# Last expert of a mixture of experts: the order in which four tiles take their gathered rows on VectorE

## The chip, the core and the metric

The kernel runs on one core of one Trainium2 chip. The time is the device time of one execution in microseconds (us); "the time" of a kernel is the median of several runs. Besides the times there is a profile: one execution recorded by the hardware profiler. Its engines are PE (TensorE matmuls), PEld (TensorE weight loads), DVE (VectorE), ACT (ScalarE), POOL (GpSimd) and SP (SyncE, which issues most DMAs).

## What is computed

One decoder layer, in float32, on 16 sequences of 256 tokens with 256 channels. Three steps, each followed by a residual sum and a layer norm: a recurrence over time with a gated state, an attention of the tokens over a context of 77 rows and themselves, and a mixture of experts. Only the last matters here:

```python
weights = _router(x, expert_embeddings)
ones = (weights > 0).astype(weights.dtype)
cap_ones = jnp.where(jnp.cumsum(ones, axis=0) <= expert_capacity, ones, 0.0)
caw = weights * cap_ones
vals, idx = jax.lax.top_k(caw.T, expert_capacity)
index = idx.reshape(-1)
x_flat = x.reshape(n_tokens, hidden)
tokens = x_flat[index].reshape(E, expert_capacity, hidden)
inter = jax.nn.relu(jnp.einsum('ech,eih->eci', tokens, first_linear))
out = jnp.einsum('eci,ehi->ech', inter, second_linear)
out = out * vals[:, :, None]
final = jnp.zeros((n_tokens, hidden), x.dtype).at[index].add(out.reshape(-1, hidden))
```

The router's weights are a softmax over each token's best 2 of 8 experts, and an expert takes at most 512 rows. A token has up to two experts. Its output row is the layer norm of its input row plus the weighted results of both.

## The kernel before

The attention takes most of the span; the experts come at the end, in a loop of nine turns (lines 1394 to 1415). Turns 0 and 1 belong to expert 0 (four tiles of 128 rows, and two more), turns 2 to 8 to experts 1 to 7 with four tiles each. `LAST` is 8. Each turn has these parts:

- The token rows were put into a DRAM buffer `xg`, sorted by expert. `Rows(e)` (line 1144) loads a turn's rows, and `read` (line 1157) works out, for every row, the weight `w`, whether another expert's result joins it (`joins`), where that lies (`at`), and to which output row it goes (`to`; out of bounds where a later expert finishes the token).
- `turn_rows` (line 1227) transposes the rows on PE, `first_product` (line 1240) makes the hidden layer in four matmul groups, with ScalarE's Relu (line 1255).
- `second_product` (line 1264) makes 128 x 256 of output for each tile with four accumulated matmuls (line 1275). In turns before the last, ScalarE scales each by its weight (line 1285), and for every two tiles SP stores them into the DRAM buffer `oe` (line 1288), from which later experts' turns gather them. In the last turn, VectorE instead first puts "input row plus joined row" of all four tiles into `y` (line 1271, through `add_other`, line 1262), and then adds each product with its weight (line 1283). Its tiles 2 and 3 have PSUM banks of their own (`pk`, `pq`).
- `gather(e + 1)` (line 1305) issues, on POOL, one indirect DMA for each tile of the next turn (line 1310). It reads what this turn stored, so the first waits for that store.
- `finish` (line 1318) takes the tiles in groups: statistics (line 1334) and aggregate (line 1335) of each tile, variance plus epsilon (line 1338), `root` (line 1291: ScalarE's square root at line 1294, then four small VectorE instructions that take the reciprocal and refine it, lines 1296 to 1302), the scaling of each tile (line 1342), and one indirect DMA for each tile to the output, issued by POOL (line 1343). In the last turn the groups are tiles 0 and 1, tile 2, tile 3.

The order on each engine is made when the program is built. The framework gives every engine a queue of its own; what is traced earlier goes first if it is ready by the builder's estimate, otherwise something later may take its place. `with tc.issue_after(ins):` is the means to constrain that: what is traced in the block is queued behind `ins`. Line 1410 uses it in turn 7: its `finish` stands in a block behind the last gather of turn 8.

Of the kernel before, what the change touches and what calls it, by code (L numbers as in the profile page):

```python
# [10 lines left out]
F32 = mybir.dt.float32  # L11
I32 = mybir.dt.int32
AF = mybir.ActivationFunctionType
ALU = mybir.AluOpType
# [4 lines left out]
P = 128  # L19
B, S, D = 16, 256, 256  # L20
# [18 lines left out]
def decoder_layer(  # L39
# [29 lines left out]
    V, A, G, T = nc.vector, nc.scalar, nc.gpsimd, nc.tensor  # L69
# [5 lines left out]
    NS = CAP // P  # L75
# [8 lines left out]
    def bank(name, tag="mm", bufs=2):  # L84
        return ps.tile([P, 512], F32, tag=tag, bufs=bufs, name=name)
# [40 lines left out]
    def apart(group, dma):  # L126

        for other in groups.get(group, []):
            tc.declare_no_dep(dma.ins, other.ins, reason="disjoint rows")
        groups.setdefault(group, []).append(dma)  # L130
# [3 lines left out]
    def rsqrt(v, n, rows, name):  # L134
        r = small.tile([P, n], F32, tag="r", name=f"r{name}")
        powers.append(G.tensor_tensor(r[:rows], v[:rows], nhalf[:rows, 0:n], ALU.pow))
        return r
# [674 lines left out]
    rows, xets = {}, {}  # L812
# [322 lines left out]
    LAST = E  # L1135
    SLOTS = [(0, 0, NS), (0, CAP, GT)] + [(e, FIRST[e], NS) for e in range(1, E)]
# [90 lines left out]
    def turn_rows(e):  # L1227
        x, n = rows[e].x, rows[e].n
        xet = e0.tile([P, DC, CAP], F32, tag="xet", bufs=2, name=f"xet{e}")
        for k in range(DC):  # L1230
            pt = bank(f"pe{e}_{k}", "pk" if k == 0 else "pq", 1)
            for s in range(n):
                T.transpose(pt[:, s * P : (s + 1) * P], x[:, s, k * P : (k + 1) * P], ident)  # L1233
            if k == 0:
                V.tensor_copy(xet[:, k, 0 : n * P], pt[:, 0 : n * P])
            else:
                A.copy(xet[:, k, 0 : n * P], pt[:, 0 : n * P])
        xets[e] = xet

    def first_product(e):  # L1240
        xet, w1, c = xets.pop(e), w1_s[SLOTS[e][0]], SLOTS[e][2] * P
        it = e0.tile([P, NF, CAP], F32, tag="it", name=f"it{e}")
        for f in range(NF):
            if f == 0:
                two = ps.tile([P, 2, 512], F32, tag="s", bufs=1, name=f"pi{e}")
            pi = two[:, f, :] if f < 2 else bank(f"pi{e}_{f}", "pa" if f == 2 else "po", 1)
            for k in range(DC):
                T.matmul(  # L1248
                    pi[:, 0:c],
                    lhsT=w1[:, k, f * P : (f + 1) * P],  # L1250
                    rhs=xet[:, k, 0:c],
                    start=(k == 0),
                    stop=(k == DC - 1),
                )
            A.activation(it[:, f, 0:c], pi[:, 0:c], AF.Relu)
        return it

    gs, ys = {}, {}

    def add_other(e, s, dst, src):  # L1260

        V.scalar_tensor_tensor(dst, gs[e][:, s, :], rows[e].joins[:, s : s + 1], src, ALU.mult, ALU.add)

    def second_product(e, it, tiles):
        if tiles[0] == 0:
            ys[e] = e2.tile([P, NS, D], F32, tag="ye", name=f"ye{e}")
        y = ys[e]
        w2 = w2_s[SLOTS[e][0]]
        if e == LAST and tiles[0] == 0:
            for s in range(NS):  # L1270
                add_other(e, s, y[:, s, :], rows[e].x[:, s, 0:D])
        for s in tiles:
            po = bank(f"pf{e}_{s}") if e < LAST or s < 2 else bank(f"pf{e}_{s}", ("pk", "pq")[s - 2], 1)
            for f in range(NF):
                T.matmul(  # L1275
                    po[:, 0:D],
                    lhsT=it[:, f, s * P : (s + 1) * P],
                    rhs=w2[:, f, :],
                    start=(f == 0),
                    stop=(f == NF - 1),  # L1280
                )
            if e == LAST:
                V.scalar_tensor_tensor(y[:, s, :], po[:, 0:D], rows[e].w[:, s : s + 1], y[:, s, :], ALU.mult, ALU.add)  # L1283
                continue
            A.activation(y[:, s, :], po[:, 0:D], AF.Copy, scale=rows[e].w[:, s : s + 1])  # L1285
            if s % 2 == 1:
                r0 = SLOTS[e][1] + (s - 1) * P
                nc.sync.dma_start(oe_d[r0 : r0 + 2 * P, :].rearrange("(i p) d -> p i d", p=P), y[:, s - 1 : s + 1, :])
        return y

    def root(v, n, name):

        q = es.tile([P, n], F32, tag="qe", name=f"qe{name}")
        A.activation(q, v, AF.Sqrt)
        i0 = es.tile([P, n], F32, tag="ie", name=f"ie{name}")
        V.reciprocal(i0, q)
        i2 = es.tile([P, n], F32, tag="i2", name=f"i2{name}")
        V.tensor_tensor(i2, i0, i0, ALU.mult)
        t = es.tile([P, n], F32, tag="te", name=f"te{name}")
        V.scalar_tensor_tensor(t, i2, -0.5, v, ALU.mult, ALU.mult)  # L1300
        r = es.tile([P, n], F32, tag="re", name=f"re{name}")
        V.scalar_tensor_tensor(r, t, 1.5, i0, ALU.add, ALU.mult)
        return r

    def gather(e):

        R = rows[e]
        gs[e] = e2.tile([P, NS, D], F32, tag="ge", name=f"ge{e}")
        for s in range(R.n):
            last = G.indirect_dma_start(  # L1310
                out=gs[e][:, s, :],
                out_offset=None,
                in_=oe_d[0 : SLOTS[e][1], :],
                in_offset=bass.IndirectOffsetOnAxis(ap=R.at[:, s : s + 1], axis=0),
            )
        return last

    def finish(e, y):
        R = rows[e]
        mv = es.tile([P, NS, 2], F32, tag="mve", name=f"mve{e}")  # L1320
        o = e2.tile([P, NS, D], F32, tag="oe", name=f"oe{e}")
        us = {}
        for a, z in [(0, 2), (2, 3), (3, 4)] if e == LAST else [(a, a + 2) for a in range(0, R.n, 2)]:
            for s in range(a, z):
                if e == LAST:
                    u = y[:, s, :]
                else:
                    u = es.tile([P, D], F32, tag="u", name=f"ue{e}_{s}")
                    V.tensor_tensor(u, R.x[:, s, 0:D], y[:, s, :], ALU.add)
                    if e > 1:  # L1330
                        add_other(e, s, u, u)
                us[s] = u
                st = small.tile([P, 6], F32, tag="st", name=f"ste{e}_{s}")
                V.bn_stats(st, u)  # L1334
                V.bn_aggr(mv[:, s, :], st)  # L1335
            n = z - a
            v = small.tile([P, n], F32, tag="v", name=f"ve{e}_{a}")
            V.tensor_scalar(v, mv[:, a:z, 1], EPS, None, ALU.add)
            r = rsqrt(v, n, P, f"e{e}_{a}") if e == 0 else root(v, n, f"{e}_{a}")
            for s in range(a, z):  # L1340
                i = slice(s - a, s - a + 1)
                V.tensor_scalar(o[:, s, :], us[s], mv[:, s, 0:1], r[:, i], ALU.subtract, ALU.mult)  # L1342
                dma = G.indirect_dma_start(  # L1343
                    out=out_f,
                    out_offset=bass.IndirectOffsetOnAxis(ap=R.to[:, s : s + 1], axis=0),
                    in_=o[:, s, :],
                    in_offset=None,
                    bounds_check=N - 1,
                    oob_is_err=False,
                )  # L1350
                apart("out", dma)


    heads = [(b, h) for b in range(B) for h in range(H)]
# [36 lines left out]
    e2 = ctx.enter_context(tc.tile_pool(name="e2", bufs=2))  # L1391
    load_expert(1, e2)
    load_expert(2, e2)
    for e in range(LAST + 1):
        it = first_product(e)
        if e < LAST:
            rows[e + 1] = Rows(e + 1)
            rows[e + 1].read(e + 1)

        tiles = list(range(SLOTS[e][2]))  # L1400
        ahead = 1 if e == 1 else 0
        if ahead:
            second_product(e, it, tiles[:ahead])
        if 0 < e < LAST:
            turn_rows(e + 1)
        y = second_product(e, it, tiles[ahead:])
        gathered = gather(e + 1) if 0 < e < LAST else None
        if e == LAST - 1:

            with tc.issue_after(gathered.ins):  # L1410
                finish(e, y)
        else:
            finish(e, y)
        if 2 <= e < E - 1:
            load_expert(e + 1, e2)

# [49 lines left out]
```

## Time and profile before

| what | value |
|---|---|
| time, median of 3 runs | 1169.77 us |
| the three runs | 1169.77, 1172.89, 1169.11 us |
| the profiled execution's own time | 1171.0 us |
| its span | 1169.3 us |
| granted TensorE clock, mean | 0.997 |
| DVE busy, of the span | 782.1 us (67%) |
| POOL busy, of the span | 316.1 us (27%) |
| turn 8's second matmuls (line 1275) | 1151.94 to 1159.01 us |
| turn 8's four gather issues (line 1310) start | 1149.04, 1150.31, 1151.57, 1152.82 us |
| turn 7's four output issues (line 1343) start | 1154.07, 1155.39, 1156.69, 1157.97 us |
| turn 8's four output issues start | 1161.39, 1162.66, 1163.94, 1165.22 us |

Positions are microseconds from the start of the span. The profiled execution's own time is a little above its span, by what lies around the recorded instructions. A row of the timeline gives the start, the length, the engine, the line, the operation, and output and inputs by the names of the program; in brackets stands the idle time of that engine before it, and what ended it. "issue" there means that the engine waited for nothing that the profile shows. The chain of work that ended last is followed back from the last instruction: each piece is what released the next one.

### The profile page before, as it was taken

How to read it: one execution, taken by the hardware profiler on the slowest of the kernel's cores; microseconds unless marked ns; L12 is line 12 of the kernel's file. 1: busy time of each engine (PE TensorE's matmuls, PEld its weight loads, DVE VectorE, ACT ScalarE, POOL GpSimd, SP SyncE). 2: the span in 40 equal slices, each digit the busy share in tenths (PEclk: the TensorE clock that was granted, in tenths of full speed). 3: DMA queues.
4: the chain of work that ended last, by engine and by line, in shares of the span. 5: the costliest groups of instructions: out<-in, count | busy, mean ns of one | idle time of the engine just before them, and what ended most of it. 6: DMA issues, size and time to landing. Idle time of an engine off the chain costs nothing. (4 is left out here: it accounts for less than half of the span.)

```text
span 1169.3 us, 16020 instructions
## 1 busy us (share of the span) xinstructions
PE 1135.1 (97%) x5380; PEld 821.0 (70%) x5380; DVE 782.1 (67%) x2144; ACT 499.0 (43%) x1315; POOL 316.1 (27%) x565
## 2 busy tenths in 40 slices
PE   7999999999999999999999999999999999999996
PEld 3465676767787777677777777777777778876664
DVE  6655877676657776777567757865567555665666
ACT  3344444453444344444444444444444444523331
POOL 2201241114210530242015302340142014144455
PEclk9999999999999999999999999999999999999998
DMA  8741010001000110010000100000001000046652
GB/s 276 206 128 39 20 38 18 11 28 58 19 12 10 54 36 12 28 40 19 12 10 27 37 11 10 18 19 12 10 17 46 20 10 15 21 159 138 181 160 90
DMA packets 47417, 60.63 MB, mean 52 GB/s; under 512 B 7957, under 2 KB 37374, under 8 KB 47336
## 3 DMA queue, kind: packets, MB, share of 16 engines
q1 hardware_dynamic: 39686, 50.18, 14.1%
q0 software_dynamic: 6048, 9.22, 3.3%
q8 instruction: 42, 0.69, 0.2%
q10 hardware_dynamic: 1602, 0.23, 0.1%
q14 instruction: 39, 0.32, 0.1%
HBM read 36.33 MB, written 30.78 MB: 57 GB/s over the span
## 5 line engine op out<-in xcount | busy, mean ns | idle before, releaser
L660 PE MATMUL po<-ptt,v 128*128 128x256 f32 (+1 forms) x768 | 189.2, 381 | 1.6 <-DVE rs L632 1.6
L660 PEld LDWEIGHTS po<-ptt,v 128*128 128x128 f32 (+1 forms) x768 | 142.0, 190 | 51.7 <-issue 34.4
L609 PE MATMUL pk<-kvt,wkv_s 128*128 128x333 f32 x512 | 165.4, 444 | 0.0
L624 PE MATMUL s<-kt,qt 128*128 128x333 f32 x512 | 164.5, 443 | 0.0
L626 DVE TENSOR_REDUCE nm<-s 128x2 f32<-128x666 f32 x128 | 108.3, 846 | 72.1 <-PE s L624 68.1
L630 ACT ACTIVATE p<-s,nm 128x333 f32<-128x333 f32 x256 | 135.7, 536 | 44.5 <-DVE nm L626 44.2
L614 PE MATMUL pq<-kvt,wq_s 128*128 128x256 f32 x512 | 131.2, 378 | 0.0
L609 PEld LDWEIGHTS pk<-kvt,wkv_s 128*128 128x128 f32 x512 | 91.1, 191 | 45.6 <-issue 22.9
L668 ACT ACTIVATE ot<-po,bkv_s 128x256 f32<-128x256 f32 x128 | 60.9, 476 | 140.3 <-PE po L660 135.7
L624 PEld LDWEIGHTS s<-kt,qt 128*128 128x128 f32 x512 | 96.3, 188 | 31.6 <-issue 1.3
L614 PEld LDWEIGHTS pq<-kvt,wq_s 128*128 128x128 f32 x512 | 96.7, 189 | 30.8 <-issue 1.0
L649 ACT COPY ptt<-pb 77x256 f32<-77x256 f32 x128 | 47.3, 369 | 164.1 <-PE pb L646 161.0
L634 DVE TENSOR_SCALAR p<-p,rs 128x333 f32<-128x333 f32 x256 | 98.5, 421 | 3.3
L990 POOL DMA_INDIRECT xg<-xs,sidx x64 | 66.1, 1032 | 98.3 <-ACT ot L668 38.9
L648 DVE COPY ptt<-pa 128x512 f32<-128x512 f32 x128 | 87.3, 682 | 0.7 <-PE pa L646 0.7
L646 PEld LDWEIGHTS pa<-ident,p 128*128 128x128 f32 x512 | 63.9, 141 | 29.3
L611 ACT ACTIVATE kt<-pk,bkv_s 128x333 f32<-128x333 f32 x128 | 69.1, 540 | 28.2 <-PE pk L609 21.7
L646 PE MATMUL pa<-ident,p 128*128 128x128 f32 x512 | 76.8, 273 | 0.0
L351 DVE SCALAR_TENSOR_TENSOR cv<-hp,cw,cv 128x512 f32<-128x512 f32 (+1 forms) x108 | 74.1, 692 | 1.6
L616 ACT ACTIVATE qt<-pq,bqs 128x256 f32<-128x256 f32 x128 | 61.1, 478 | 20.2 <-PE pq L614 15.3
L336 PE MATMUL ph<-xT,inw 128*128 128x512 f32 (+1 forms) x144 | 63.1, 567 | 5.5 <-DMA inw<-in_in_wT 4.4
L1275 PE MATMUL pf<-w,it 128*128 128x256 f32 x272 | 61.3, 381 | 2.0 <-ACT ye L1285 1.7
(264 smaller groups left out, 1764.6 us busy)
## 6 DMA issues: line engine op xcount, KB each, us to landing
v<-vc SPq DMA_DIRECT2D x16, 308.0 KB
xg<-zero SPq DMA_DIRECT2D x34, 131.0 KB
xe<-xg SPq DMA_DIRECT2D x8, 524.0 KB
xt<-in_x_in SPq DMA_DIRECT2D x16, 256.0 KB
out<-o SPq DMA_DIRECT2D x16, 256.0 KB
w<-in_w1T SPq DMA_DIRECT2D x8, 512.0 KB
w<-in_w2T SPq DMA_DIRECT2D x8, 512.0 KB
oe<-ye SPq DMA_DIRECT2D x15, 256.0 KB
```

Source lines behind the costliest of these rows:

```text
L351: conv = V.scalar_tensor_tensor(cv, hp[:, :, k : k + S], cw[:, c, k : k + 1], cv, ALU.mult, ALU.add)
L609: T.matmul(pk[:, 0:J], lhsT=wkv_s[:, k, f], rhs=kvt[:, k, :], start=(k == 0), stop=(k == DC - 1))
L611: A.activation(kt, pk[:, 0:J], AF.Identity, bias=bkv_s[:, h : h + 1])
L614: T.matmul(pq[:, 0:S], lhsT=wq_s[:, k, f], rhs=kvt[:, k, 0:S], start=(k == 0), stop=(k == DC - 1))
L624: T.matmul(s[:, ic, 0:J], lhsT=qt[:, ic * P : (ic + 1) * P], rhs=kt, start=True, stop=True)
L626: V.tensor_reduce(nm, s[:, :, 0:J], AX.X, ALU.max, negate=True)
L630: A.activation(p[:, ic, :], s[:, ic, 0:J], AF.Exp, bias=nm[:, ic : ic + 1], accum_out=sm[:, ic : ic + 1])
L634: V.tensor_scalar(p[:, ic, :], p[:, ic, :], rs[:, ic : ic + 1], None, ALU.mult)
L646: T.transpose(dst[0:jn, c0 : c0 + P], pn[:, ic, j0 : j0 + jn], ident)
L648: turned = V.tensor_copy(ptt[:, 0:2, :], pt01.rearrange("p (j i) -> p j i", j=2))
L660: T.matmul(po[:, 0:S], lhsT=vs[b][0:jn, jc, h * DH : (h + 1) * DH], rhs=ptt[0:jn, jc, :], start=(jc == 0), stop=(jc == 2),)
L990: dma = G.indirect_dma_start(out=xg[:, :], out_offset=bass.IndirectOffsetOnAxis(ap=sidx[:, t, c : c + 1], axis=0), in_=xs[b + t // GT][:, ...
```

## The change

In the last turn, VectorE's work is laid out in another order. The "input row plus joined row" is made for tiles 0 and 1 alone; then the second product of these two and their `finish` are traced. That of tiles 2 and 3 is queued behind the aggregate of tile 1 (`known`). The second product and the `finish` of tile 2 and then of tile 3 stand in a block that is queued behind the scaling of tile 1 (`scaled`). For that, `finish` takes its groups of tiles as an argument and returns the two instructions, and its tiles are kept between its calls. The other turns get the same groups as before. No instruction is added or taken away.

```diff
     def second_product(e, it, tiles):
-        if tiles[0] == 0:
+        if tiles[0] == 0 and e < LAST:
             ys[e] = e2.tile([P, NS, D], F32, tag="ye", name=f"ye{e}")
         y = ys[e]
         w2 = w2_s[SLOTS[e][0]]
-        if e == LAST and tiles[0] == 0:
-            for s in range(NS):
-                add_other(e, s, y[:, s, :], rows[e].x[:, s, 0:D])
         for s in tiles:
...
-    def finish(e, y):
+    ends_of = {}
+
+    def finish(e, y, groups_of_tiles):
         R = rows[e]
-        mv = es.tile([P, NS, 2], F32, tag="mve", name=f"mve{e}")
-        o = e2.tile([P, NS, D], F32, tag="oe", name=f"oe{e}")
+        if groups_of_tiles[0][0] == 0:
+            ends_of[e] = (
+                es.tile([P, NS, 2], F32, tag="mve", name=f"mve{e}"),
+                e2.tile([P, NS, D], F32, tag="oe", name=f"oe{e}"),
+            )
+        mv, o = ends_of[e]
         us = {}
-        for a, z in [(0, 2), (2, 3), (3, 4)] if e == LAST else [(a, a + 2) for a in range(0, R.n, 2)]:
+        for a, z in groups_of_tiles:
...
-                V.bn_aggr(mv[:, s, :], st)
+                known = V.bn_aggr(mv[:, s, :], st)
...
-                V.tensor_scalar(o[:, s, :], us[s], mv[:, s, 0:1], r[:, i], ALU.subtract, ALU.mult)
+                scaled = V.tensor_scalar(o[:, s, :], us[s], mv[:, s, 0:1], r[:, i], ALU.subtract, ALU.mult)
...
+        return known, scaled
...
+        if e == LAST:
+
+            y = ys[e] = e2.tile([P, NS, D], F32, tag="ye", name=f"ye{e}")
+            other = lambda s: add_other(e, s, y[:, s, :], rows[e].x[:, s, 0:D])
+            other(0)
+            other(1)
+            second_product(e, it, [0, 1])
+            known, scaled = finish(e, y, [(0, 2)])
+            with tc.issue_after(known.ins):
+                other(2)
+                other(3)
+            with tc.issue_after(scaled.ins):
+                for s in (2, 3):
+                    second_product(e, it, [s])
+                    finish(e, y, [(s, s + 1)])
+            break
...
-        gathered = gather(e + 1) if 0 < e < LAST else None
+        gathered = gather(e + 1) if e > 0 else None
+        pairs_of = [(a, a + 2) for a in range(0, SLOTS[e][2], 2)]
         if e == LAST - 1:
 
             with tc.issue_after(gathered.ins):
-                finish(e, y)
+                finish(e, y, pairs_of)
         else:
-            finish(e, y)
+            finish(e, y, pairs_of)
```

## The prediction

> **What bounds the kernel now.** I read the page first, then the chain of work that ended last from 1140 us on, then the timeline of the same stretch, then the waits and the table of stretches.
>
> ```profile
> PE 1135.1 (97%) x5380; PEld 821.0 (70%) x5380; DVE 782.1 (67%) x2144; ACT 499.0 (43%) x1315; POOL 316.1 (27%) x565
> ```
>
> TensorE (PE) is busy for 97% of the span, so nearly all the time is its queue, and the change adds and removes no matmul. What can move is only the stretch behind the last matmul. The chain shows what sets it (start, length):
>
> ```profile
> 1152.82 3.44 DMA ge<-oe,at
> 1156.26 0.02 issue
> 1156.28 0.04 DVE ye L1262
> 1156.32 0.37 issue
> 1156.68 0.49 DVE ye L1283
> ...
> 1163.94 0.98 POOL out L1343
> 1164.92 1.28 POOLq L1462
> ```
>
> From 1152.82 the chain isn't on PE: it waits for the fourth gather, then runs on VectorE (DVE), then through the output DMAs that GpSimd (POOL) issues. The timeline gives the order (start, length, engine, line; in brackets the idle time before it):
>
> ```profile
> 1151.84 0.48 DVE L1262 SCALAR_TENSOR_TENSOR ye<-ge,joins,xe 128x256 f32<-128x256 f32 x1 [1.40 <-DMA ge<-oe,at]
> 1151.94 7.07 PE L1275 MATMUL pf<-w,it 128*128 128x256 f32 x32
> ...
> 1153.12 0.48 DVE L1262 SCALAR_TENSOR_TENSOR ye<-ge,joins,xe 128x256 f32<-128x256 f32 x1 [0.80 <-DMA ge<-oe,at]
> ...
> 1154.85 0.48 DVE L1262 SCALAR_TENSOR_TENSOR ye<-ge,joins,xe 128x256 f32<-128x256 f32 x1 [1.24 <-DMA ge<-oe,at]
> ...
> 1156.28 0.48 DVE L1262 SCALAR_TENSOR_TENSOR ye<-ge,joins,xe 128x256 f32<-128x256 f32 x1 [0.95 <-DMA ge<-oe,at]
> 1156.68 0.48 DVE L1283 SCALAR_TENSOR_TENSOR ye<-pf,we,ye 128x256 f32<-128x256 f32 x1
> ...
> 1157.97 0.97 POOL L1343 DMA_INDIRECT out<-oe,to  x1 [0.30 <-issue]
> ...
> 1161.39 0.97 POOL L1343 DMA_INDIRECT out<-oe,to  x1 [2.44 <-DVE oe L1342]
> ...
> 1165.22 0.97 POOL L1343 DMA_INDIRECT out<-oe,to  x1 [0.30 <-issue]
> ```
>
> Call the four L1262 instructions adds 0 to 3, those of L1283 combines 0 to 3. All four adds stand ahead of combine 0, so tile 0, whose own gather was in at 1151.84, waits until 1156.28 for tile 3's. The table of stretches prices it (length, then busy PE, PEld and DVE):
>
> ```profile
> 1154.07:1156.28 2.21, 2.21 (x12) 1.93 (x12) 0.48 (x1) 0.00 (x0) 1.90 (x2) 1.00 0.41 113
> 1161.39:1164.41 3.02, 0.00 (x0) 0.00 (x0) 2.84 (x16) 0.41 (x2) 2.41 (x3) 0.61 0.20 73
> ```
>
> DVE idles while PE works, and is nearly full once PE is done. POOL idled 2.44 us before the first of the last four output issues, and then the four follow 1.28 us apart (0.98 and 0.30 between): 1161.39 + 3 x 1.28 = 1165.23. So the end is "first output issue plus three pitches"; the last scaling (oe, L1342), done at 1164.41, was 0.5 us early for its issue.
>
> **The change, part by part.**
>
> *Python only.* The moved allocations, `ends_of`, the returned handles, `pairs_of` and `gather` under `e > 0` issue nothing: turn 0 still gathers nothing, turns 1 to 7 do as before. Cost 0, with nothing needed to hide it.
>
> *What the ordering binds.* The trace shows it at line 1410, where turn 7's finish is queued behind the last gather: its POOL issues waited until 1154.07, behind the gathers (1149.04 to 1153.77), while DVE instructions of the same block ran from 1140.45. So only the engine of the named instruction is bound, here DVE. PE's matmuls for tiles 2 and 3 should keep their place.
>
> *When the products can be taken.* Turn 7's second matmuls began at 1138.01 and ScalarE took its tiles at 1139.94, 1141.67, 1143.40 and 1145.64: 1.93, 3.66, 5.39 and 7.63 after. Turn 8's begin at 1151.94: 1153.87, 1155.60, 1157.33, 1159.57. Combines 0 and 1 now wait for PE, which they didn't. Price of that wait: at least 0, at most the 0.5 by which turn 7's fourth tile ran late. I take 0, since the first three were evenly 1.73 apart.
>
> *Tiles 0 and 1 (moved forward).* From rows of before, start to start: combine to statistics 0.52 (1156.68 to 1157.20), statistics to aggregate 0.46, aggregate to ve (L1338) 0.21. Tile 0: 1153.87, 1154.39, 1154.85. Tile 1: 1155.60, 1156.12, 1156.58. This last is `known`. ve follows at 1156.79.
>
> *Adds 2 and 3 (moved back).* They come behind `known`; their gathers were in at 1154.85 and 1156.28, so they wait for no DMA. Each occupies DVE for 0.40 (1159.64 to 1160.04 for an instruction of their shape). The price has two ends. If they fill the holes of the root: from ve to the first scaling takes 1.40 with nothing between (1162.60 to 1164.00), and 1.80 with two instructions of 128x256 and small ones between (1158.92 to 1160.72). If both stand ahead of ve: 0.90 and then 1.40, 0.29 more in all (scaling at 1158.88). I take the fill, since turns 6 and 7 and turn 8 itself were laid out so. First scaling: 1156.79 + 1.80 = 1158.59.
>
> *Tiles 2 and 3 (queued behind the scaling).* Waiting behind it on DVE are combines 2 and 3, their statistics and scalings; through them ScalarE's two roots and two output issues. The next combine follows the first scaling by 0.69 (1160.72 to 1161.41): combine 2 at 1159.28 (before: 1159.64), its product two us old. ve of tile 2: 0.52 + 0.46 + 0.21 later, 1160.47; combine 3 another 0.06 on (1161.35 to 1161.41): 1160.53. From combine 3 I copy the old tail: scaling 2 ended 1.89 after it (1163.30), scaling 3 3.00 after it (1164.41). New: 1162.42 and 1163.53.
>
> *POOL.* Turn 7's outputs still end at 1158.94; the first issue is free from 1159.24, and scaling 0 (done 1158.95) plus the 0.30 pitch gap gives 1159.25. Second 1160.53. Third 1162.42 + 0.30 = 1162.72. Fourth the later of 1163.83 and 1162.72 + 1.28: 1164.00. Before: 1165.22. Sum: -1.22 us. The start from 1165.22 to the span's end, 4.08 us of issue and landing, is kept.
>
> So the stall of 4.4 us before the adds doesn't come back whole: about 2 us of it become work for two tiles, the rest is spent waiting for tile 1's product and on the two adds, now in the crowded part; the bound passes from POOL's pitch to DVE's work for tiles 2 and 3.
>
> *A rule against it.* The new DVE work from 1153.87 lies beside POOL's output issues of turn 7. The Trainium skill (SBUF — State Buffer, sections "SBUF: two separate sides" and "A bandwidth-pool intuition that's wrong (but worth ruling out)") says that GpSimd can't write its DMA descriptors while VectorE runs certain two-port instructions, and gives 620 ns becoming 3100. Were turn 7's four issues held 2.5 us each, the first output of turn 8 would start some 10 us later, about 1169, and the kernel be slower by 8. The trace disagrees for these forms: the gather issues at 1140.82 and 1142.07 ran beside adds (two inputs in SBUF) and took 0.94 and 0.95, and outputs take 0.97 to 1.01; the single long one, 1.25 at 1133.46, lies beside such work too. Even 0.27 on each of the four puts the first output at 1160.33 and the fourth at 1164.17 by pitch, 0.17 later than my sum. I take 0.
>
> **The rivals.**
>
> 1. *My forecast, filled holes* (chance 0.60): -1.22, with adds ahead of ve -0.93. Profiled span 1169.3 to 1168.1, that execution 1171.0 to 1169.8. The median of before is 1169.77, 1.2 below the profiled execution: 1168.55, rounded 1168.6.
>
> 2. *More* (0.10): only PE's end and POOL's pitch bind. Tile 3 visible at 1159.57, then 0.52 + 0.46 + 0.21 + 1.40 + 0.41 + 0.30 gives 1162.87; four pitches from 1159.25 give 1163.09. So -2.1 at most, 1167.6. Against it: DVE has more than that to do for tiles 2 and 3.
>
> 3. *Nothing comes of it* (0.17): tile 1's product late by 0.5, adds ahead of ve (0.3) and an output issue at 1.25 leave -0.3 or so; or the order isn't changed where it counts. Within 0.4 of 1169.8.
>
> 4. *Slower: tiles 2 and 3 in series* (0.11). The queue takes from DVE the work that filled its holes. If tile 3 follows only after tile 2's whole chain, each takes 0.52 + 0.46 + 0.21 + 1.40 + 0.41 = 3.00: 1159.28 + 6.00 = 1165.28, issue 1165.58, +0.36; with the adds ahead of ve +0.65, so 1170.1 to 1170.4. It decides once scaling 3 ends after 1164.92, that is when 1.4 us of overlap are lost. For it: the tiles are traced one after the other. Against it: in turns 6 to 8 other tiles' instructions do stand in the holes.
>
> 5. *The ordering holds PE too* (0.02): matmuls for tile 2 start at 1159.28, tile 3 is visible 3.66 later at 1162.94, +3.00 + 0.30 = 1166.24: +1.0, 1170.8. Line 1410's trace speaks against it.
>
> **How the numbers follow.** About 0.3%, 3.5 us, is what a measurement of this kernel can tell from no change. None of the cases reaches it: even the best is 2.1, the worst 1.0. Outside lie only a disturbance of the time itself (one of the three runs of before was 3.1 above the median) and something that no row shows, the port rule among it: 0.02 faster, 0.05 slower, 0.93 within. The range goes from the bound of case 2, 1167.6, to case 5 less a little, 1170.6, which also leaves room for a median that is some tenths off; below and above remain about 0.08 and 0.12.
>
> **What would show it.** Right: combine 0 near 1153.9 and ended-by PE, not by a gather; adds 2 and 3 between ve and the first scaling; first output issue near 1159.3, directly behind turn 7's last, with idle time of POOL now before the third; the fourth near 1164.0; PE's last matmul still at 1159.0. Wrong: combine 1 after 1156; adds 2 and 3 ahead of ve; combine 3 behind scaling 2 (case 4); PE idle between tiles 1 and 2 (case 5); output issues of turn 7 longer than 1.1 us (the port rule). Anything that differs before 1150 would be none of my steps.

## The result and the profile after

Over 20 runs each, the median went from 1171.04 us (1168.13 to 1173.54) to 1173.12 us (1171.05 to 1177.11): ratio 1.0016, interval 1.0009 to 1.0024. That is slower by 1.9 us by the ratio, 2.1 by the medians. It is less than the 0.3% that the forecast took for no change, but the interval is clear of 1, it lies on the other side of no change than the predicted -1.2 us, and 1173.12 lies above the forecast's range of 1167.6 to 1170.6. An occasion, below, is a set of runs made together. The later runs fell on two kinds of occasion, told apart by their traces: PE's products came in time or late. So every ratio here compares runs of one occasion, and positions are given as "us after turn 8's first second matmul".

| | before | after |
|---|---|---|
| profiled execution, its span | 1171.0, 1169.3 us | 1173.65, 1171.9 us |
| first of turn 8's second matmuls | 1151.94 | 1152.50 |
| fourth output issue, after that | 13.28 us | 15.38 us |

The span grew by 2.6 us. Of that, 0.56 is the later start of the matmuls, upstream of the edit (of the stretches from one turn's second matmuls to the next, only that from turn 6 to turn 7 differs by more than 0.2: 15.36 against 14.81 us). The share that lies behind it, where the edit acts, is 15.38 - 13.28 = 2.10 us. The page's first line shows as much work as before:

```profile
PE 1135.4 (97%) x5380; PEld 821.0 (70%) x5380; DVE 781.5 (67%) x2144; ACT 497.0 (42%) x1315; POOL 316.1 (27%) x565
```

The timeline of the end of the changed kernel (start, length, engine, line; in brackets the idle time before and what ended it):

```profile
1152.50 7.07 PE L1272 MATMUL pf<-w,it 128*128 128x256 f32 x32
...
1154.43 0.48 DVE L1280 SCALAR_TENSOR_TENSOR ye<-pf,we,ye 128x256 f32<-128x256 f32 x1 [0.80 <-PE pf L1272]
...
1156.17 0.48 DVE L1280 SCALAR_TENSOR_TENSOR ye<-pf,we,ye 128x256 f32<-128x256 f32 x1 [0.58 <-PE pf L1272]
...
1157.25 0.45 DVE L1262 SCALAR_TENSOR_TENSOR ye<-ge,joins,xe 128x256 f32<-128x256 f32 x1
1157.62 0.16 DVE L1341 TENSOR_SCALAR ve<-mve 128x2 f32<-128x2 f32 x1
1157.69 0.48 DVE L1262 SCALAR_TENSOR_TENSOR ye<-ge,joins,xe 128x256 f32<-128x256 f32 x1
...
1157.99 1.02 POOL L1346 DMA_INDIRECT out<-oe,to  x1 [0.30 <-issue]
...
1158.87 0.73 DVE L1345 TENSOR_SCALAR oe<-ye,mve,re 128x256 f32<-128x256 f32 x2
1159.56 0.97 POOL L1346 DMA_INDIRECT out<-oe,to  x1 [0.54 <-issue]
1160.49 0.48 DVE L1280 SCALAR_TENSOR_TENSOR ye<-pf,we,ye 128x256 f32<-128x256 f32 x1 [0.89 <-PE pf L1272]
1160.83 0.97 POOL L1346 DMA_INDIRECT out<-oe,to  x1 [0.30 <-issue]
1163.39 0.48 DVE L1280 SCALAR_TENSOR_TENSOR ye<-pf,we,ye 128x256 f32<-128x256 f32 x1 [2.41 <-remote]
1163.79 0.74 DVE L1337 BATCH_NORM_STATS2 ste<-ye 128x6 f32<-128x256 f32 x2
...
1166.61 0.97 POOL L1346 DMA_INDIRECT out<-oe,to  x1 [4.80 <-DVE oe L1345]
1167.88 0.97 POOL L1346 DMA_INDIRECT out<-oe,to  x1 [0.30 <-issue]
```

Up to the first output issue (1159.56) all stands within 0.3 us of where the forecast put it. Combine 2 (1160.49, at 7.99) is already 0.65 later than the forecast's 7.34 and waits 0.89 us for PE. Then DVE stops for 2.41 us ahead of combine 3 (1163.39), though PE's last matmul is on record as ended at 1152.50 + 7.07 = 1159.57. "remote" means that the row names no releaser; combine 3's only input that isn't long there is PE's product. Tile 2's statistics come behind combine 3, together with tile 3's (x2), and the third output issue comes after 4.80 us of idle time on POOL, when their scaling is done. The table of stretches shows the hole (length, then busy PE, PEld, DVE, ACT and POOL with counts, clock, DMA share, GB/s):

```profile
1162.00:1163.00 1.00, 0.00 (x0) 0.00 (x0) 0.00 (x0) 0.00 (x0) 0.00 (x0) 0.68 0.37 131
1163.00:1164.00 1.00, 0.00 (x0) 0.00 (x0) 0.61 (x2) 0.00 (x0) 0.00 (x0) 0.50 0.00 0
```

From 1162 to 1163 no engine works, only DMAs move. They belong to turn 8's second output: the first has landed at 1161.90, the second at 1163.09, and 0.3 us later combine 3 starts. The trace also records when an engine's semaphore (the counter by which one engine tells the others that it is done) is updated. PE's update for tile 3, its "signal" below, is recorded at 1163.36; combine 3 starts 0.03 later. The end of a matmul's row is modelled and not observed, but the last matmul's start is on record too, 6.69 us after the first, in this trace as in one with signals in time. So the lateness lies behind that start; whether the product itself or only its signal was late, no record tells.

### The profile page after: what moved, and what is told of

It reads as the page before. It is cut to its first block, busy times and chain, and to the rows that moved or that the text cites. A ratio compares the mean times of both kernels' runs of the same rounds, so it can differ in the third digit from the quotient of the medians.

```text
span 1171.9 us, 16020 instructions
## 1 busy us (share of the span) xinstructions
PE 1135.4 (97%) x5380; PEld 821.0 (70%) x5380; DVE 781.5 (67%) x2144; ACT 497.0 (42%) x1315; POOL 316.1 (27%) x565
```

## Theories

- **H, held signal.** On some occasions PE's signal that a tile is finished reaches its consumer only about when the indirect DMAs that GpSimd has in flight at that time have landed. The matmul rows don't show it. The change sends turn 8's first two outputs before tile 3's signal is there, so the signal waits for their landing as well.
- **Q, queueing.** The new order itself costs: what is queued behind the scaling, and tile 2's statistics behind combine 3, come later whatever PE does.
- **Nothing of the edit.** The difference is a run-to-run shift, like the 0.56 upstream.

## The experiments

All kernels below are the changed one with one edit more, if nothing else is said.

**First set: take away or hold back what is in flight.** Two kernels leave output issues out: those of turn 8's tiles 0 and 1, and those of turn 7.

```diff
+                if e == LAST and s < 2:      # in the second kernel: e == LAST - 1
+                    continue
                 dma = G.indirect_dma_start(
```

> The changed kernel without the two output DMAs of tiles 0 and 1 in turn 8; those rows of the output are left unwritten, all else is as before. In the changed kernel combine 2 began 7.99 us and combine 3 10.89 us after the first of turn 8's second matmuls, though the last matmul's record ended at 7.07. Theory H (products are held back: VectorE is told late of a finished matmul group while output DMAs are in flight): combine 2 at about 8.0 or sooner (turn 7's outputs are still there), combine 3 at 8.6 or sooner, as in the kernel before, where PE's signal came at 8.58. Theory Q (the last two products come late on their own, as they are the last of PE's queue or because of VectorE's own order): combines 2 and 3 stay at 8.0 and 10.9.

> The changed kernel without the four output DMAs of turn 7, whose rows are left unwritten. Theory H: combine 2 follows directly on the scaling of tiles 0 and 1, with no wait for PE, since nothing is in flight while tile 2 ends; combine 3 is still held, to about 2.5 us after the second of turn 8's output issues begins. Theory Q: combine 2 waits to 8.0 us and combine 3 to 10.9 us after the first second matmul, as in the changed kernel.

A third holds tiles 0's and 1's output issues back until combine 3 is done (`apart_out` issues an output as before, `taken[3]` is combine 3), and a fourth sends these two through SP, as plain transfers to a scratch buffer:

```diff
-                dma = G.indirect_dma_start(
...
+                held = lambda s=s: apart_out(R, o, s)
+                if e == LAST and s < 2:
+                    waiting.append(held)
+                else:
+                    held()
...
+                        for one in waiting:
+                            tc.add_manual_dep(one().ins, taken[3].ins.name, ...)
```

```diff
+                if e == LAST and s < 2:
+                    nc.sync.dma_start(aside[s * P : (s + 1) * P, :], o[:, s, :])
+                    continue
```

> The changed kernel with the issues of the first two outputs of turn 8 held until combine 3 is done; the same instructions, VectorE's order as in the changed kernel. Theory H: combine 3 at 8.6 us after the first second matmul instead of 10.9, first output issue near 9.3, the four 1.28 apart, so the end about 2 us sooner than in the changed kernel and within 0.5 us of the kernel before: ratio to the kernel before 0.9995 to 1.0006. Theory Q: combine 3 stays at 10.9, the first output issue comes at 11.6 and the fourth at 15.4, so as late as in the changed kernel: ratio 1.0015 to 1.002.

> The changed kernel with the outputs of tiles 0 and 1 of turn 8 sent by SyncE's plain DMAs (128 KB each, the same bytes) to a scratch buffer in DRAM instead of GpSimd's indirect ones, so those rows of the output are left unwritten. Theory H, any transfer holds PE's products: combine 3 near 10.9 us after the first second matmul, or at the end of these transfers. Theory H, only GpSimd's indirect DMAs do: combine 3 at 8.6 or sooner, as without these outputs. Theory Q: 10.9 in any case.

Measured: without the two outputs 1166.63 us, without turn 7's 1167.24, through SP 1167.69 (one run each), held back 1166.96 beside 1168.17 of the kernel before, ratio 0.999 (0.9983 to 0.9997). In all four tile 3's signal came 7.08 us after the first second matmul, 0.01 behind the end of its matmuls on record, and combines 2 and 3 ran at 7.00 and 7.39. (The expectations count "0.4 us after the last matmul" from that matmul's start, at 6.69.) The delay was absent in the kernels that should still have had it, too, so these runs told nothing of its cause. They told something else: the kernel before was 2.9 us faster here than in the first comparison, and in turns 2 to 8 no signal of PE for a second product was late in any of the four.

**Second set: both kernels again, and each half of the change alone.** "Known only" drops the queueing behind the scaling. "Queue only" puts all four adds ahead again and keeps the queueing.

```diff
-            with tc.issue_after(scaled.ins):
-                for s in (2, 3):
-                    second_product(e, it, [s])
-                    finish(e, y, [(s, s + 1)])
+            for s in (2, 3):
+                second_product(e, it, [s])
+                finish(e, y, [(s, s + 1)])
```

```diff
-            other(0)
-            other(1)
+            for s in range(NS):
+                other(s)
...
-            with tc.issue_after(known.ins):
-                other(2)
-                other(3)
```

The changed kernel unedited:

> The changed kernel once more, unedited, beside the kernel before on the same chip. In the four runs before this one PE's signal came 0.4 us after the last matmul of every tile in the turns from 1060 us on; in the two profiles first compared it came up to 1.9 us (before) and 4.2 us (changed) late while GpSimd's indirect DMAs were in flight. Theory H (the late signals cost the changed kernel its gain; they belong to the occasion, not to the edit): with signals in time, combine 3 follows combine 2 directly behind the scaling, the fourth output issue begins near 12.0 us after the first second matmul instead of 13.3, ratio 0.9985 to 0.9995; with signals late, ratio 1.001 to 1.002 as first measured. Theory Q (the order itself costs): signals may come in time, but the ratio stays at 1.001 to 1.002.

The kernel before, against itself:

> The kernel before once more, as a profile of the same occasion and a null for the comparison: ratio within 0.9993 to 1.0007. Theory H: its profile has PE's signals in time if that of the changed kernel has; the fourth output issue begins 13.3 us after the first second matmul in either case, since no signal of PE's is waited for. Theory Q says the same.

> The changed kernel without the second queueing: tiles 2 and 3 are not queued behind the scaling, only the adds 2 and 3 behind the aggregate of tile 1. VectorE's order then has combine 2 among the small instructions of the first root, and combine 3 behind the scaling. Theory H, signals in time: about as the changed kernel, the scaling 0.4 us later, tile 3's last scaling a little sooner: ratio 0.9985 to 0.9995. Signals late: combine 2 holds up the scaling and so the first two outputs, by up to 2.6 us, ratio 1.000 to 1.002. Theory Q (the queueing behind the scaling is what costs): faster than the changed kernel by 1 us or more whatever the signals do.

> The kernel before with the second queueing alone: all four adds stand first, as before, and tiles 2 and 3 are queued behind the scaling of tile 1. The early start for tiles 0 and 1 is undone, the serial work at the end kept. Both theories: slower than the kernel before, as combine 2 and its statistics no longer fill the first root's holes: the scaling comes 0.4 us sooner, combine 3 with all its work ends about 0.3 to 1.0 us later, the fourth issue 13.4 to 14.3 us after the first second matmul: ratio 1.000 to 1.0009. If this loss is 1.5 us or more, the queueing alone explains the first result (theory Q).

Measured (kernel before: 1170.47 us, 58 runs): changed 1172.42, ratio 1.0015 (1.0007 to 1.0022); before against itself 0.9996 (0.9985 to 1.0007); known only 0.9993 (0.9985 to 1.0000); queue only 1.0003 (0.9993 to 1.0014). The slowdown is back in its old size, so "nothing of the edit" falls. Neither half shows it alone (the interval of queue only does reach 1.0014), so what costs is mainly what the two halves do together. The traces show what only the whole does: send the first two outputs before tile 3's signal. Rows of the changed kernel in this set:

```profile
1149.54 7.07 PE L1272 MATMUL pf<-w,it 128*128 128x256 f32 x32
...
1156.67 0.97 POOL L1346 DMA_INDIRECT out<-oe,to  x1 [0.46 <-issue]
...
1157.95 0.97 POOL L1346 DMA_INDIRECT out<-oe,to  x1 [0.30 <-issue]
1160.49 0.48 DVE L1280 SCALAR_TENSOR_TENSOR ye<-pf,we,ye 128x256 f32<-128x256 f32 x1 [3.10 <-remote]
...
1164.99 0.97 POOL L1346 DMA_INDIRECT out<-oe,to  x1 [0.30 <-issue]
```

And of known only:

```profile
1150.11 7.07 PE L1272 MATMUL pf<-w,it 128*128 128x256 f32 x32
...
1157.75 0.48 DVE L1280 SCALAR_TENSOR_TENSOR ye<-pf,we,ye 128x256 f32<-128x256 f32 x1 [1.91 <-PE pf L1272]
...
1159.71 0.97 POOL L1346 DMA_INDIRECT out<-oe,to  x1 [2.70 <-DVE oe L1345]
1159.75 0.46 DVE L1280 SCALAR_TENSOR_TENSOR ye<-pf,we,ye 128x256 f32<-128x256 f32 x1
...
1163.55 0.97 POOL L1346 DMA_INDIRECT out<-oe,to  x1 [0.30 <-issue]
```

The matmul rows are alike, 7.07 us. In the first, output issues stand at 1156.67 and 1157.95, and combine 3 waits 3.10 us. In the second, the first output comes at 1159.71, and combine 3 follows 0.04 later without a wait. Combine 2 waited 1.91 us for PE in this kernel, so late signals are there too; they only cost less. All six traces in which signals came late, in us after the first second matmul:

| kernel | first output issue | last landing ahead of the signal | tile 3's signal, PE's last on record | combine 3 | fourth output issue |
|---|---|---|---|---|---|
| before, first comparison | 9.44 | 8.17 | 8.58 | 9.47 | 13.28 |
| before, second set | 9.00 | 8.09 | 8.09 | 9.02 | 12.83 |
| known only | 9.61 | 8.33 | 8.38 | 9.64 | 13.44 |
| queue only | 8.53 | 8.14 | 8.20 | 9.34 | 13.55 |
| changed, first comparison | 7.06 | 10.59 | 10.86 | 10.89 | 15.38 |
| changed, second set | 7.13 | 10.66 | 10.93 | 10.95 | 15.45 |

In the first four the last landing ahead of the signal is one of turn 7's outputs; in the last two it is turn 8's second. The signal follows within 0.41 us in all six, while the matmuls end at 7.07 in all. These are single executions: the two traces of the kernel before differ by 0.45 in the fourth issue.

Two things in the same traces speak against H as it is worded. In both late traces of the changed kernel, tiles 0 and 1 came in time (combines at 1.93 and at 3.65 or 3.67) while gathers and turn 7's outputs were in flight. And tile 2's signal in the second set came at 7.34, 0.67 behind one landing (6.67) and 0.66 ahead of the next on record (8.00), with turn 7's fourth output still in flight. So a DMA in flight doesn't hold every signal, and not every late signal comes at a landing.

**Third set: does the order cost anything where signals are in time?** The changed kernel, held back, and the two that leave the outputs out or send them through SP:

> The changed kernel unedited, as the measure of this occasion. Theory H, refined by the last runs: on some occasions PE's signal of a finished tile reaches VectorE only when GpSimd's indirect DMAs that are in flight have landed; the changed kernel then has combine 3 some 10.9 us after the first second matmul and ratio 1.0015; on others the signal comes 0.4 us after the last matmul, combine 3 follows combine 2 at about 7.4, and the ratio is 0.999. Theory Q: ratio 1.0015 in both.

> The changed kernel with the first two output issues of turn 8 held until combine 3, once more, beside the changed kernel on the same occasion. Theory H: combine 3 at 8.6 or sooner whether signals are late or not (turn 7's outputs alone can delay it), ratio 0.9985 to 0.9997; if signals are late here, 1.5 us or more faster than the changed kernel. Theory Q: as slow as the changed kernel wherever that is slow.

> The changed kernel without the two output DMAs of tiles 0 and 1 in turn 8 (those rows are left unwritten), once more. Theory H: on an occasion with late signals combine 3 at 8.6 us after the first second matmul instead of 10.9; else at 7.4. Theory Q: where the changed kernel has combine 3 at 10.9, this one has too.

> The changed kernel with the outputs of tiles 0 and 1 of turn 8 sent by SyncE's plain DMAs to a scratch buffer (those rows of the output are left unwritten), once more. On an occasion with late signals: combine 3 near 8.6 if only GpSimd's indirect DMAs hold the signals, and at the landing of these transfers, 10 or later, if any transfer out of SBUF does.

> The changed kernel unedited, as the measure of this occasion: with late signals combine 3 at 10.9 us after the first second matmul and a ratio near 1.0015, with signals in time at 7.4 and a ratio near 0.9995.

> The changed kernel with the first two output issues of turn 8 held until combine 3 is done. If these two outputs cause the delay (theory H), combine 3 comes at 8.6 us or sooner on an occasion with late signals, ratio 0.9985 to 0.9997. If they only land at the same time (theory Q), combine 3 stays at 10.9, the output issues begin at 11.6, and the ratio is 1.0015 to 1.003.

> The changed kernel with these two outputs sent by SyncE's plain DMAs to a scratch buffer (those rows of the output are left unwritten). On an occasion with late signals: combine 3 at 8.6 or sooner if GpSimd's indirect DMAs alone hold the signals; at the landing of SyncE's transfers, 9.5 or later, if any transfer does.

Each kernel ran on one or both of two occasions. Measured: no late signal on either. Changed kernel 1167.32 beside 1167.64, ratio 0.9996 (0.9988 to 1.0005), and 1166.65 beside 1167.86, ratio 0.9990 (0.9982 to 0.9999); held back 0.9992 (0.9983 to 1.0000) and 0.9992 (0.9984 to 1.0000); without the two outputs 1166.60, through SP 1166.48 and 1166.64 (one run each). The end of the changed kernel on the second of these occasions:

```profile
1149.11 7.07 PE L1272 MATMUL pf<-w,it 128*128 128x256 f32 x32
...
1156.11 0.87 DVE L1280 SCALAR_TENSOR_TENSOR ye<-pf,we,ye 128x256 f32<-128x256 f32 x2
1156.15 0.97 POOL L1346 DMA_INDIRECT out<-oe,to  x1 [0.54 <-DVE oe L1345]
...
1157.42 0.97 POOL L1346 DMA_INDIRECT out<-oe,to  x1 [0.30 <-DVE ste L1337]
...
1159.72 0.97 POOL L1346 DMA_INDIRECT out<-oe,to  x1 [1.32 <-DVE oe L1345]
1161.00 0.97 POOL L1346 DMA_INDIRECT out<-oe,to  x1 [0.30 <-issue]
```

Same program, same order on every engine, same two outputs in flight; but combines 2 and 3 run together at 1156.11 without a wait, and the fourth issue stands 11.89 us after the first second matmul, where the trace of the first comparison had 15.38. So Q falls: the order costs nothing by itself. And what H says of the outputs can hold on some occasions only.

**Fourth set: catch a late occasion with the outputs held back.** The kernel that holds tiles 0's and 1's outputs back, alone, on three more occasions:

> The changed kernel with the first two output issues of turn 8 held until combine 3 is done, in search of an occasion with late signals (known by late signals of PE in turns 3 to 7 of the profile, and by 1170 us or more for the kernel before). There: theory H, combine 3 at 8.6 us or sooner after the first second matmul and ratio 0.9985 to 0.9997; theory Q, combine 3 at 10.9 and ratio 1.0015 to 1.003. On an occasion without late signals it tells nothing new: 7.4 us and 0.9992 again.

> As i_hold01, on another occasion. With late signals (kernel before 1170 us or more): theory H, combine 3 at 8.6 us or sooner after the first second matmul and ratio 0.9985 to 0.9997; theory Q, combine 3 at 10.9 and ratio 1.0015 to 1.003. Without them: 7.4 us and 0.9992.

> As i_hold01 and j_hold01, on another occasion. With late signals (kernel before 1170 us or more): theory H, combine 3 at 8.6 us or sooner after the first second matmul and ratio 0.9985 to 0.9997; theory Q, combine 3 at 10.9 and ratio 1.0015 to 1.003. Without them: 7.4 us and 0.9992, and the cause of the late signals stays open.

Measured: ratios 0.9995 (0.9986 to 1.0004), 0.9995 (0.9984 to 1.0006), 0.9998 (0.9990 to 1.0006); first output at 8.14 or 8.15, fourth at 12.06 or 12.07; signals in time in all three. The held-back kernel ran on six occasions in all, and none was a late one, so the run that would settle H didn't come about.

**What is shown, and what stays open.** Shown, on two occasions: where signals are late, the change costs 1.8 to 2.1 us. In the trace of each, combine 3 waits for PE, and tile 2's statistics, the last scalings and two outputs stand behind it. Shown: without late signals the same program isn't slower. Not shown is what makes tile 3's signal later still in the changed kernel, 10.9 where the other three have 8.1 to 8.6. That the two early outputs do it rests on the table alone, where tile 3 of six traces agrees, and no run takes the outputs away on such an occasion; tiles 0 to 2 fit only in part. So H is a lead and not a result. Whether plain transfers through SP would hold a signal stays open too. Why some occasions have late signals isn't shown either: by the records, the second set and one occasion of the fourth with signals in time ran on chips of the same number, so it needn't be the chip. Whether the recording itself takes part was not tested.

## Why the prediction was wrong, point by point

- **Tiles 0 and 1 forward, right.** Combine 0 at 1.93 us and combine 1 at 3.67 (forecast 1.93, 3.66), `known` done by 4.83; both combines released by PE, as the forecast's sign for "right" had it.
- **Adds in the holes, right but for 0.3.** Add 2 stands ahead of ve and add 3 behind it; the first scaling came at 6.37 (forecast 6.65), and with it the first output at 7.06 (7.31).
- **Only DVE is bound, right.** PE's 32 matmuls run through in 7.07 us; the case in which PE is held is out.
- **"A rule against it" at 0, right.** Turn 7's outputs took 0.97 to 1.02 beside the new DVE work.
- **Tile 2's chain ahead of combine 3, wrong.** The two tiles are laid out in pairs (statistics x2, scaling x2). From combine 3 to the fourth issue it takes 15.38 - 10.89 = 4.49 us, where the sum had 12.06 - 8.59 = 3.47: 1.02 too little. In time it didn't show: combine 3 came at 7.39 instead of 8.59, so the fourth issue stood at 11.89 against 12.06. Two errors of the working cancel there, so that agreement is in part luck.
- **The step that failed: "When the products can be taken".** The prediction read tile 2 at 5.39 and tile 3 at 7.63 from turn 7. Combine 2 had "its product two us old" at 7.34, and combine 3 stood at 8.59, so their wait for PE entered the sum as nothing. (The "at least 0, at most the 0.5" was the price for combines 0 and 1, and 0 came true there.) In the trace of the change tile 2 was to be had at 7.97 and tile 3 at 10.86, which is 3.2 later than 7.63; the two combines waited 0.89 and 2.41 us. Combine 3 at 10.89 instead of 8.59 is 2.30; with the 1.02 above, the fourth issue is 3.32 late: 12.06 + 3.32 = 15.38. What moved the signal that far stays open, as said above.
- **What the trace of before already had.** Turn 7 was a bad witness, and other turns speak against it. ScalarE's scalings of turn 5's first three products, before:

```profile
1110.06 0.48 ACT L1285 ACTIVATE ye<-pf,we 128x256 f32<-128x256 f32 x1 [1.39 <-PE pf L1275]
1112.95 0.48 ACT L1285 ACTIVATE ye<-pf,we 128x256 f32<-128x256 f32 x1 [2.42 <-PE pf L1275]
1114.43 0.48 ACT L1285 ACTIVATE ye<-pf,we 128x256 f32<-128x256 f32 x1 [1.00 <-PE pf L1275]
```

and those of the changed kernel, on the first occasion of the third set:

```profile
1106.96 0.47 ACT L1282 ACTIVATE ye<-pf,we 128x256 f32<-128x256 f32 x1 [1.15 <-PE pf L1272]
1108.69 0.47 ACT L1282 ACTIVATE ye<-pf,we 128x256 f32<-128x256 f32 x1 [1.25 <-PE pf L1272]
1110.42 0.47 ACT L1282 ACTIVATE ye<-pf,we 128x256 f32<-128x256 f32 x1 [1.25 <-PE pf L1272]
```

In time they stand 1.73 apart. In the trace of before they are 2.89 and 1.48 apart, with a wait of 2.42 for PE: late signals, to be read off before any run. The size was there as well: turn 3's second product was taken 6.32 us after that turn's first second matmul, where turn 7's stood at 3.66. And the 0.5 of turn 7's fourth tile was itself a late signal, recorded at 7.60 behind matmuls that end at 7.07.

In turn 8 of before, tile 3's signal was recorded at 1160.52 (8.58 after the first matmul), 1.5 behind the matmuls' end. DVE came to it later, so the lateness was covered; combine 3 shows no wait:

```profile
1161.41 0.48 DVE L1283 SCALAR_TENSOR_TENSOR ye<-pf,we,ye 128x256 f32<-128x256 f32 x1
```

The change takes that cover away, since DVE is done with combine 2 at 8.47. But this alone would cost only 0.1 us, had the signal stayed at 8.58: the other 2.3 of the wait come from the signal's own move to 10.86. The change also moves two output issues ahead of the signal. Their price on POOL was counted; what they might hold up was not asked.
- **The rivals.** "Slower: tiles 2 and 3 in series" got the sign, by luck, but not the mechanism: the tiles ran as a pair. The forecast's own case came true, within what could be measured, on occasions without late signals: its end at 11.89 for 12.06, and a ratio of 0.9990 and 0.9996 for the 0.9990 that -1.22 us would be. (In "More", 1163.09 is three pitches behind 1159.25, not four.)
- **The level.** The forecast's 1168.6 stood on a median of three runs, 1169.77. Twenty runs gave 1171.04 for the same kernel, so 1.3 us of the miss of 4.5 is that, and the rest is the difference between -1.2 and +2.1.

## What to carry to other kernels

When an edit lets an engine come to a product earlier, price its wait by the starts of that product's consumers in every comparable turn, not by the end of the matmul's row and not by the most even turn. Before a transfer is issued earlier, list the signals that are still pending then, and who waits for them. And ask whether work that doesn't need the late tile can stand ahead of it on the engine: here two tiles' statistics and two outputs waited for one tile. An order with tile 2's statistics ahead of combine 3 and the queueing kept was not run.

No version here is shown to be the faster one on both kinds of occasion. Holding the two outputs back measured 0.9990 to 0.9998 in time, like the change; known only, 0.9993, was faster than the changed kernel (1.0015) where signals came late, and was not run where they come in time.

## What the runs showed of the hardware

- PE's rows can be identical while the products are to be had at quite different times: in turn 8, 32 matmuls in 7.07 us in every trace, tile 3's signal at 7.08 us in time, at 8.1 to 8.6 and at 10.9 late.
- Late and in time are far apart: in turns 2 to 8 of each of the six late traces, a consumer of a second product waited for PE more than 0.25 us past the end of that tile's matmuls 8 to 12 times; in the fourteen others, never.
- Another engine's signal kept its time on a late occasion: POOL's first output issue follows the start of DVE's scaling by 0.69 us in the late trace shown first (1158.87 to 1159.56) as in the one with signals in time (1155.46 to 1156.15).
- On occasions with late signals the trace holds fewer semaphore updates, not only PE's: 1165 to 1173 of PE's where those in time have 1225, and 8263 to 8316 in all where those in time have 9694 to 9702 (9634 to 9665 without some outputs). The landing of one of turn 7's outputs is recorded as 16 updates in time and as 1 to 7 late. Whether updates come together there or are only missing from the record isn't shown. The way from turn 3's to turn 4's second matmuls takes up to 16.6 us late and 14.8 in time. The kernel before then measures 1170.5 and 1171.0 us; in time, over six occasions, 1167.6 to 1168.2.
- An indirect output of 128 rows took GpSimd 0.97 to 1.02 us to issue in the last two turns of the two traces first compared, and with nothing else to wait for each started 1.28 to 1.32 us after the one before. In the changed kernel the two at 7.06 and 8.34 landed at 9.40 and 10.59, so some 2.3 us after the start of their issue.
